# The last 48 units of a gated feed-forward layer in three PSUM banks instead of four, with TensorE adding up the four quarters of the hidden units

## The chip, the core and the metric

The kernel runs on one core of a Trainium2 chip. The metric is the device time of one execution, in microseconds (us). The kernel before takes 1150.86 us, the median of three runs from 1150.69 to 1151.08.

A core has TensorE (PE in the profile: matrix products, whose results go to PSUM, eight banks of 512 f32 columns by 128 partitions), VectorE (DVE), ScalarE (ACT), GpSimd (POOL) and DMA queues, which SyncE (SP) and GpSimd feed here. Each engine works through its own list of instructions in the order written and waits for the others by semaphores.

## What is computed

The input x has 4096 rows (2 x 2048) of 1024 f32 values. Cut to what matters:

```python
xn = layernorm(x)
# attention part: autocorrelation of each row, its 6 largest lags, softmax,
# weighted sum of the row rolled by these lags
f = rfft(xn); corr = irfft(f * conj(f)); w, delay = top_k(corr, 6)
s = sum_k softmax(w)_k * roll(xn, -delay_k)
# feed-forward part; each weight matrix is a quarter, repeated four times
lin(x, wq, A, B) = x @ tile(wq, (1, 4)).T + 0.5 * (x @ A.T) @ B.T     # LoRA of rank 2
h = silu(lin(xn, w1q, a1, b1)) * lin(xn, w3q, a3, b3)                 # 2752 units
g = silu(lin(h, w2q, a2, b2))
out = x + s * g
```

The hidden layer has 2752 units, four quarters of 688. Because w2 repeats its quarter four times, the second layer needs only the sum of the four quarters of h (688 values), and beside it the two LoRA values h @ a2.T, which need every quarter by itself.

## The kernel before

The rows are worked through in eight macros of 512 rows. Inside a macro the rows are the columns of all matrix products (512 wide), and the units are the rows. A quarter's 688 units are five chunks of 128 and a rest of 48; the chunk number c is 0 to 4, and FULL = 5 names the rest. An f32 product counts as two passes on TensorE, and the profile shows two matmuls for each.

A macro has 15 steps (STEPS). The order on every engine is written out by hand: `plan` hangs the work of the next macro's autocorrelation and of the gathers (rolled rows, fetched by GpSimd's indirect DMAs, summed by VectorE) into slots named pre, mid, half, end and between of each step, and the main loop calls them around the feed-forward code. No scheduler reorders it.

- Steps 0 to 9 (`up`): for chunk c and quarter j, a gate and an up product, each of two contraction halves (k = 0 and 1), into a bank each. A bank is seeded beforehand by ScalarE (`seed`) with the second LoRA value times its coefficient; the first LoRA value rides in the contraction itself, in row 0 of yT (gate) or yU (up), which differ in that row alone. ScalarE takes silu of the gate (L573), VectorE multiplies by the up bank (L575) into a tile z, GpSimd adds the four quarters' z into zf[c] (L578, L580).
- `a2` (L551) is LoRA's second product: for each quarter j, lhsT of 2 columns, into partitions 32j and 32j + 1 of the one bank u2. It is kept in the list `late` and issued at the next flush, one step later.
- Step 10 (`up_rest`): the rest of 48 units, below.
- Steps 11 to 14 (`down_head`, `down_tail`, twice): the output products from zf[0] to zf[4], arranged as sums and differences of blocks (`mix`, `forms`), and at the end of each half `rest` (L662): two 64-row products that add zf[5], which holds the rest's sum and the LoRA values, once in partitions 0 to 63 and again in 64 to 127. `out` follows: silu, product with s, addition of x, output DMA.

The rest before: each quarter j has its own bank of 128 rows. Rows 0 to 63 belong to the gate and 64 to 127 to the up product; of each 64, two are empty at the top, 48 are units and the others are zero. The contraction half k = 1 is the same input for both, so one 128-column product (L597) does it. Half k = 0 takes yT for the gate and yU for the up product, so it is two 64-column products into the two halves of the bank (L604). Quarters 0 and 1 come first, then the flush (a2 of chunk 4) and the slots mid and half (the next macro's last spectrum products), then quarters 2 and 3, and then four silus (L614) and four products on 64 partitions (L615). GpSimd adds three quarters (L619, L620). `a2` of the rest (64 rows, 2 columns, four quarters) is flushed in `down_head`.

`lora_mid`, at the end of step 11, finishes zf[5]: VectorE adds the fourth quarter (L625), then four times half a row pair of u2 into rows 0 and 1 (L627), and ScalarE copies the 64 rows into the upper partitions (L630). In that slot it stands behind the next macro's `again` and `lora_spread`, whose ScalarE copies are L278, L264, L272 and L273, after the TensorE product L262.

Seeds of the rest: two ScalarE instructions on 64 rows for each bank (L539), eight in a macro. The banks of `full` rotate through five buffers, shared by the gate and up banks, the rest's banks and the output banks y. The lines that say how a rest bank is seeded and used:

```python
            if c == FULL:
                acc = full(f"gu_{self.m}_{c}_{j}")
                for wi in range(2):
                    at = slice(64 * wi, 64 * wi + 64)
                    nc.scalar.activation(acc[at, :], self.st.second[at, wi, :], AF.Copy, scale=b5_sb[at, j : j + 1])
```

Of the kernel before, what the change touches and what calls it, by code (L numbers as in the profile page):

```python
# [35 lines left out]
F32 = mybir.dt.float32  # L36
U32 = mybir.dt.uint32
I32 = mybir.dt.int32
AF = mybir.ActivationFunctionType
ALU = mybir.AluOpType  # L40
# [4 lines left out]
Q2 = H // 4  # L45
TOP = 6
EPS = 1e-5
P = 128
RT = 4
NR = RT * P  # L50
NC = 6
# [4 lines left out]

FULL = 5
REST = Q2 - FULL * P
QF = FULL * P

MID = 2 * FULL
# [7 lines left out]
def block_kernel(ctx: ExitStack, tc: tile.TileContext, x, w13t, w0t, w5t, w2t, a13, b13, b5, a2t, tf, ti, pick, out):  # L69
    nc = tc.nc  # L70
    rows = x.shape[0]
# [6 lines left out]
    const = pool("const", 1)  # L78
# [3 lines left out]
    p5 = pool("p5", ROLLS)  # L82
# [21 lines left out]
    tf_sb = const.tile([P, 8, P], F32)  # L104
    ti_sb = const.tile([P, 4, NL], F32)
    w13_sb = const.tile([P, FULL, 8, 2, P], F32)
    w5_sb = const.tile([P, 2, 4, P], F32)
    w2_sb = const.tile([P, NC, L], F32)
    t_sb = const.tile([P, 3, 2, 512], F32)
    b5_sb = const.tile([P, 4], F32)  # L110
    b13_sb = const.tile([P, FULL, 8], F32)
    a2_sb = const.tile([P, 4 * NC, 2], F32)
    a13_sb = const.tile([P, 8, 32], F32)
    pick_sb = const.tile([P, P], F32)

# [24 lines left out]
    def lessen(w, w0):  # L140

        nc.vector.scalar_tensor_tensor(w(0), w0, minus, w(0), ALU.mult, ALU.add)
        nc.gpsimd.tensor_tensor(w(1), w(1), w0, ALU.subtract)
# [338 lines left out]
    class Gathers:  # L482
# [3 lines left out]
        def add(self, st, r):  # L486
            self.ready += [(st, r, k) for k in range(TOP)]
# [30 lines left out]
    class Ffn:  # L518
# [13 lines left out]
        def seed(self, i, which=(0, 1)):  # L532

            c, j = divmod(i, 4)
            if c == FULL:
                acc = full(f"gu_{self.m}_{c}_{j}")
                for wi in range(2):
                    at = slice(64 * wi, 64 * wi + 64)
                    nc.scalar.activation(acc[at, :], self.st.second[at, wi, :], AF.Copy, scale=b5_sb[at, j : j + 1])  # L539
                self.accs[i] = acc  # L540
            if c >= FULL:
                return
            for wi in which:
                acc = full(f"gu_{self.m}_{c}_{j}_{wi}")
                q = 2 * j + wi
                nc.scalar.activation(acc, self.st.second[:, wi, :], AF.Copy, scale=b13_sb[:, c, q : q + 1])  # L546
                self.accs.setdefault(i, []).append(acc)

        def a2(self, c, zs, rows):
            for j, z in enumerate(zs):  # L550
                nc.tensor.matmul(  # L551
                    self.u2[32 * j : 32 * j + 2, :], lhsT=a2_sb[:rows, 4 * c + j, :], rhs=z[:rows, :],
                    start=(c == 0), stop=(c == FULL),
                )

        def flush(self):
# [3 lines left out]
        def up(self, c, pair, mid, half):  # L560
            zs, st = self.zs.setdefault(c, []), self.st
            for jj in range(2):
                j = 2 * pair + jj
                accs = self.accs.pop(4 * c + j)
                for wi, acc in enumerate(accs):
                    for k in range(2):
                        y = (st.yT[:, 0, :], st.yU)[wi] if k == 0 else st.yT[:, 1, :]
                        nc.tensor.matmul(  # L568
                            acc, lhsT=w13_sb[:, c, 2 * j + wi, k, :], rhs=y, start=False, stop=(k == 1),
                            skip_group_check=True,  # L570
                        )
                z = p5.tile([P, NR], F32, tag="z", name=f"z_{self.m}_{c}_{j}")
                nc.scalar.activation(z, accs[0], AF.Silu)  # L573
                self.seed(4 * c + j + 2)
                nc.vector.tensor_tensor(z, z, accs[1], ALU.mult)  # L575
                zs.append(z)
                if j == 1:
                    nc.gpsimd.tensor_tensor(self.sum_of(c), zs[0], zs[1], ALU.add)  # L578
                elif j > 1:
                    nc.gpsimd.tensor_tensor(self.zf[c], self.zf[c], z, ALU.add)  # L580
                if jj == 0:
                    self.flush()
                    mid()
                    half()
            if pair == 1:
                self.late.append(lambda: self.a2(c, zs, P))

        def up_rest(self, mid, half):

            st = self.st  # L590
            self.seed(4 * FULL + 2)
            self.seed(4 * FULL + 3)
            accs = [self.accs.pop(4 * FULL + j) for j in range(4)]
            for pair in range(2):
                js = (2 * pair, 2 * pair + 1)
                for j in js:
                    nc.tensor.matmul(  # L597
                        accs[j], lhsT=w5_sb[:, 1, j, :], rhs=st.yT[:, 1, :], start=False, stop=False, skip_group_check=True
                    )

                for j in js:
                    for wi, y in enumerate((st.yT[:, 0, :], st.yU)):
                        at = slice(64 * wi, 64 * wi + 64)
                        nc.tensor.matmul(  # L604
                            accs[j][at, :], lhsT=w5_sb[:, 0, j, at], rhs=y, start=False, stop=True, skip_group_check=True
                        )
                if pair == 0:
                    self.flush()
                    mid()
                    half()  # L610
            zs = self.zs[FULL] = []
            for j, acc in enumerate(accs):
                z = p5.tile([P, NR], F32, tag="z", name=f"z_{self.m}_{FULL}_{j}")
                nc.scalar.activation(z[:64, :], acc[:64, :], AF.Silu)  # L614
                nc.vector.tensor_tensor(z[:64, :], z[:64, :], acc[64:, :], ALU.mult)  # L615
                zs.append(z)
            self.late.append(lambda: self.a2(FULL, zs, 64))
            last = self.sum_of(FULL)
            nc.gpsimd.tensor_tensor(last[:64, :], zs[0][:64, :], zs[1][:64, :], ALU.add)  # L619
            nc.gpsimd.tensor_tensor(last[:64, :], last[:64, :], zs[2][:64, :], ALU.add)  # L620

        def lora_mid(self):

            last, z = self.zf[FULL], self.zs[FULL][3]
            nc.vector.tensor_tensor(last[:64, :], last[:64, :], z[:64, :], ALU.add)  # L625
            for j in range(4):
                nc.vector.scalar_tensor_tensor(  # L627
                    last[0:2, :], self.u2[32 * j : 32 * j + 2, :], 0.5, last[0:2, :], ALU.mult, ALU.add
                )
            nc.scalar.copy(last[64:, :], last[:64, :])  # L630

        def mix(self, a):
# [174 lines left out]
    def load_first(c):  # L807
        w0 = first_times[c] = p3.tile([P, 8, P], F32, tag="s", name=f"w0_{c}")
        if c < FULL:
            nc.sync.dma_start(w0, bass.AP(w0t.tensor, w0t.offset + c * 8 * P, [[0, P], [P, 8], [1, P]]))  # L810
        else:
            nc.sync.dma_start(w0[:, :4, :], bass.AP(w0t.tensor, w0t.offset + c * 8 * P, [[0, P], [P, 4], [1, P]]))

    def lessen_part(c):
        w0 = first_times.pop(c)
        if c < FULL:
            lessen(lambda k: w13_sb[:, c, :, k, :], w0)
        else:
            lessen(lambda k: w5_sb[:, k, :, :], w0[:, :4, :])


    with tc.manual_schedule():
# [70 lines left out]


        st.lora_first(ffns[0])
        for m in range(macros):
            ffn = ffns[m]
            ffn.start()
            pre, mid, half, end, sums, between = plan(m, corrs[m], corrs[m + 1], corrs[m + 2], gathers, ffns[m + 1])
            for p in range(STEPS):  # L900
                for f in pre[p]:
                    f()
                gathers.begin()
                middle = lambda p=p: [f() for f in mid[p]]

                def others(p=p):
                    gathers.sum(sums[p][0])
                    if sums[p][0]:
                        gathers.begin()
                    for f in half[p]:  # L910
                        f()

                if p < MID:
                    ffn.up(p // 2, p % 2, middle, others)
                elif p == MID:
                    ffn.up_rest(middle, others)
                else:
                    q, part = divmod(p - MID - 1, 2)
                    if part == 0:
                        ffn.down_head(q, middle, others)  # L920
                    else:
                        s = lambda i, q=q: gathers.whole(m, 2 * q + i)
                        ffn.down_tail(middle, others, s, lambda p=p: [f() for f in between[p]])
                gathers.sum(sums[p][1])
                for f in end[p]:
                    f()
# [111 lines left out]
```

## Time and profile before

| | us |
|---|---|
| median of three runs | 1150.86 |
| profiled execution | 1149.63 |
| its span (first to last instruction) | 1147.6 |
| mean granted TensorE clock | 0.993 of full speed |
| TensorE busy | 1110.5 |
| VectorE busy | 832.1 |
| GpSimd busy | 718.7 |
| ScalarE busy | 617.4 |

The two passes of an f32 product appear as two matmuls. In the profile's timeline each line gives the start, the length, the engine, the line of the kernel, the operation, the tile written and the tiles read, the shape of the weights (rows*columns) and the count of instructions merged. The profile draws a matmul from its start until its last result is written, so that neighbours overlap: how fast TensorE goes is read from the distance of starts.

The costliest lines on TensorE are L568 (the chunks' gate and up products) and L652 (the output products). The lines of the rest are small: L597 x64 (30.2 us), L604 x128 (30.9 us in shared passes), and L551 on the rest x64 (8.3 us).

### The profile page before, as it was taken

How to read it: one execution, taken by the hardware profiler on the slowest of the kernel's cores; microseconds unless marked ns; L12 is line 12 of the kernel's file. 1: busy time of each engine (PE TensorE's matmuls, PEld its weight loads, DVE VectorE, ACT ScalarE, POOL GpSimd, SP SyncE). 2: the span in 40 equal slices, each digit the busy share in tenths (PEclk: the TensorE clock that was granted, in tenths of full speed). 3: DMA queues.
4: the chain of work that ended last, by engine and by line, in shares of the span. 5: the costliest groups of instructions: out<-in, count | busy, mean ns of one | idle time of the engine just before them, and what ended most of it. 6: DMA issues, size and time to landing. Idle time of an engine off the chain costs nothing.

```text
span 1147.6 us, 11271 instructions
## 1 busy us (share of the span) xinstructions
PE 1110.5 (97%) x3476; PEld 472.8 (41%) x3476; DVE 832.1 (73%) x1213; ACT 617.4 (54%) x1077; POOL 718.7 (63%) x607
## 2 busy tenths in 40 slices
PE   5988799999999999999999999999999999999997
PEld 4433234443444434444344443444344443444432
DVE  5689788777777777778767777777777777763563
ACT  4736453666437663476635665366643766345541
POOL 4577774778366773578635784567836677356832
PEclk9998999999999999999999999999999999999999
DMA  9942555565355652556435663555635565154533
GB/s 363 417 142 74 165 174 172 186 212 200 109 176 204 214 183 67 194 207 214 157 101 204 218 201 101 167 179 207 199 110 176 202 218 180 52 182 131 160 95 119
DMA packets 64915, 201.77 MB, mean 176 GB/s; under 512 B 7612, under 2 KB 7868, under 8 KB 64088
## 3 DMA queue, kind: packets, MB, share of 16 engines
q0 software_dynamic: 27648, 100.68, 28.1%
q1 hardware_dynamic: 37208, 100.39, 24.0%
q8 instruction: 27, 0.44, 0.1%
q14 instruction: 32, 0.26, 0.1%
HBM read 150.65 MB, written 50.39 MB: 175 GB/s over the span
## 4 chain that ended last, share of the span: by engine, by line
PE 86%; DVE 4%; POOL 4%; issue 3%; DMA 1%; ACT 1%; SPq 0%; DVEq 0%; POOLq 0%; ACTq 0%
PE gu L568 44%; PE y L652 19%; PE u L551 4%; PE y L662 3%; PE gu L604 2%; PE gu L597 2%; PE t L234 2%; PE fe L385 1%; PE fo L385 1%; PE o L432 1%; PE fe L388 1%; PE e L432 1%; PE fo L388 1%; PE ua L250 1%; DMA x<-in_x 1%
## 5 line engine op out<-in xcount | busy, mean ns | idle before, releaser
L568 PE MATMUL gu<-yT,w_sb 128*128 128x512 f32 x960 | 461.4, 602 | 1.4 <-ACT gu L546 1.4
L568 PEld LDWEIGHTS gu<-yT,w_sb 128*128 128x128 f32 x960 | 177.0, 191 | 236.2 <-issue 211.7
L493 POOL DMA_INDIRECT roll<-scr,lag x192 | 233.4, 1216 | 42.8 <-issue 30.3
L515 DVE SCALAR_TENSOR_TENSOR s<-roll,w,s 128x1024 f32<-128x1024 f32 x160 | 229.1, 1432 | 5.0 <-DMA roll<-scr,lag 4.1
L546 ACT ACTIVATE gu<-second,b_sb 128x512 f32<-128x512 f32 x320 | 208.4, 685 | 9.6 <-DVE z L575 8.0
L575 DVE TENSOR_TENSOR z<-z,gu 128x512 f32<-128x512 f32 x160 | 108.9, 683 | 116.9 <-PE gu L568 80.4
L580 POOL TENSOR_TENSOR zf<-zf,z 128x512 f32<-128x512 f32 x80 | 129.5, 1619 | 67.1 <-DVE z L575 66.1
L573 ACT ACTIVATE z<-gu 128x512 f32<-128x512 f32 x160 | 95.1, 594 | 141.6 <-PE gu L568 138.8
L568 PE MATMUL gu<-yU,w_sb 128*128 128x512 f32 x320 | 163.4, 592 | 0.0
L468 POOL TENSOR_TENSOR e<-euler,e 128x6 f32<-128x6 f32 x32 | 49.6, 1549 | 150.2 <-DVE e L467 135.4
L652 PE MATMUL y<-w_sb,zf 128*128 128x512 f32 x256 | 122.1, 599 | 0.0
L734 POOL TENSOR_TENSOR x<-g,x 128x512 f32<-128x512 f32 x62 | 81.4, 1322 | 61.6 <-DVE g L733 37.5
L568 PEld LDWEIGHTS gu<-yU,w_sb 128*128 128x128 f32 x320 | 61.1, 191 | 77.4 <-issue 69.9
L578 POOL TENSOR_TENSOR zf<-z,z 128x512 f32<-128x512 f32 x40 | 64.8, 1621 | 29.9 <-DVE z L575 29.6
L733 DVE TENSOR_TENSOR g<-s,g 128x512 f32<-128x512 f32 x64 | 52.7, 853 | 39.5 <-ACT g L732 38.7
L732 ACT ACTIVATE g<-y 128x512 f32<-128x512 f32 x64 | 35.4, 593 | 73.5 <-PE y L662 40.8
L652 PEld LDWEIGHTS y<-w_sb,zf 128*128 128x128 f32 x256 | 46.2, 190 | 59.8 <-issue 59.0
L450 ACT COPY corr<-corr 128x511 f32<-128x511 f32 x32 | 19.8, 617 | 85.2 <-DVE corr L449 85.2
L652 PE MATMUL y<-w_sb,S 128*128 128x512 f32 x128 | 61.8, 605 | 0.0
L652 PE MATMUL y<-t_sb,zf 128*128 128x512 f32 x128 | 60.2, 592 | 0.0
L210 DVE TENSOR_TENSOR a<-x 128x512 f32<-128x512 f32 x28 | 34.9, 1246 | 26.2 <-ACT x L203 26.2
L551 PE MATMUL u<-z,a_sb 128*2 128x512 f32 (+1 forms) x384 | 50.9, 591 | 0.5 <-DVE z L575 0.5
(181 smaller groups left out, 1534.1 us busy)
## 6 DMA issues: line engine op xcount, KB each, us to landing
scr<-x SPq DMA_DIRECT2D x64, 512.0 KB
x<-in_x SPq DMA_DIRECT2D x32, 512.0 KB
x<-in_x SPq DMA_DIRECT2D x64, 256.0 KB
out<-x SPq DMA_DIRECT2D x64, 256.0 KB
w_sb<-in_w13t SPq DMA_DIRECT2D x5, 1024.0 KB
second<-rows SPq DMA_DIRECT2D x14, 256.0 KB
w_sb<-in_w2t SPq DMA_DIRECT2D x1, 3072.0 KB
roll<-scr,lag POOLq DMA_INDIRECT x192, 5.2
```

Source lines behind the costliest of these rows:

```text
L493: nc.gpsimd.indirect_dma_start(out=g, out_offset=None, in_=st.scratch[r].rearrange("p (n o) -> (p n) o", o=1), in_offset=bass.IndirectOffs ...
L515: nc.vector.scalar_tensor_tensor(s, g, w, s, ALU.mult, ALU.add)
L546: nc.scalar.activation(acc, self.st.second[:, wi, :], AF.Copy, scale=b13_sb[:, c, q : q + 1])
L551: nc.tensor.matmul(self.u2[32 * j : 32 * j + 2, :], lhsT=a2_sb[:rows, 4 * c + j, :], rhs=z[:rows, :], start=(c == 0), stop=(c == FULL),)
L568: nc.tensor.matmul(acc, lhsT=w13_sb[:, c, 2 * j + wi, k, :], rhs=y, start=False, stop=(k == 1), skip_group_check=True,)
L573: nc.scalar.activation(z, accs[0], AF.Silu)
L575: nc.vector.tensor_tensor(z, z, accs[1], ALU.mult)
L578: nc.gpsimd.tensor_tensor(self.sum_of(c), zs[0], zs[1], ALU.add)
L580: nc.gpsimd.tensor_tensor(self.zf[c], self.zf[c], z, ALU.add)
L652: nc.tensor.matmul(acc, lhsT=lhs, rhs=rhs, start=(first and a == 0), stop=True, skip_group_check=True)
L733: nc.vector.tensor_tensor(g, s(i)[:, cols], g, ALU.mult)
L734: (nc.vector if last else nc.gpsimd).tensor_tensor(xt, g, xt, ALU.add)
```

## The change

The 48 units of all four quarters are dealt out anew. The first 32 of each quarter (HEAD) make 4 x 32 = 128 rows: one full bank for the gate and one for the up product. The last 16 of each quarter (TAIL) make 64 rows: the gate's in partitions 0 to 63 and the up product's in 64 to 127 of a third bank. So there are three banks, `gate`, `up` and `last`.

`up_rest` does gate and up with four full products, then silu on 128 rows and one VectorE product into the tile `head`; then the flush and the slots as before; then `last` with one full product and two 64-column ones, silu and product on 64 rows into `tail`.

The quarters are no longer added by GpSimd. LoRA's second product for the rest (`a2_rest`) is two products of 64 columns: head (128 rows) into partitions 0 to 63 of u2, tail (64 rows) into 64 to 127. Besides the two LoRA columns, their weights hold a 2.0 for each unit in the column of its sum; all of a2_sb is scaled by 0.5 once, at setup, by ScalarE. To have all of u2's 128 rows written, `a2` on chunk 0 has 32 columns for each quarter instead of 2, with zeros in the others. Tile shapes on TensorE, as the program has them: 128 rows by 64 columns for head, 64 by 64 for tail, 64 by 32 for each of the four products before.

`lora_mid` becomes: ScalarE copies the upper half of u2 into zf[5], VectorE adds the lower half of u2 to it, ScalarE copies the result into the upper partitions. Rows 32 and 33 of each 64 now carry the LoRA values of other quarters, so w2's rows for the rest hold b2 twice.

Seeds: one ScalarE instruction each for gate and up, two for `last`. Loads: a2 grows from 24 to 144 KB, w5 shrinks from 512 to 384 KB, its correction w0 from 256 to 192 KB.

```diff
+HEAD = 32
+TAIL = REST - HEAD
...
-    w5_sb = const.tile([P, 2, 4, P], F32)
+    w5_sb = const.tile([P, 2, 3, P], F32)
...
-    a2_sb = const.tile([P, 4 * NC, 2], F32)
+    a2_sb = const.tile([P, 288], F32)
...
-            if c == FULL:
+            if c == FULL and j < 3:
                 acc = full(f"gu_{self.m}_{c}_{j}")
-                for wi in range(2):
-                    at = slice(64 * wi, 64 * wi + 64)
+                for wi, at in ((0, slice(0, 64)), (1, slice(64, P))) if j == 2 else ((j, slice(0, P)),):
                     nc.scalar.activation(acc[at, :], self.st.second[at, wi, :], AF.Copy, scale=b5_sb[at, j : j + 1])
...
-        def a2(self, c, zs, rows):
+        def a2(self, c, zs):
             for j, z in enumerate(zs):
+                n, at = (32, 32 * j) if c == 0 else (2, 4 * 32 + 8 * (c - 1) + 2 * j)
                 nc.tensor.matmul(
-                    self.u2[32 * j : 32 * j + 2, :], lhsT=a2_sb[:rows, 4 * c + j, :], rhs=z[:rows, :],
-                    start=(c == 0), stop=(c == FULL),
+                    self.u2[32 * j : 32 * j + n, :], lhsT=a2_sb[:, at : at + n], rhs=z,
+                    start=(c == 0), stop=True, skip_group_check=True,
+                )
+
+        def a2_rest(self, zs):
+
+            for z, rows, at in zip(zs, (P, 64), (0, 64)):
+                nc.tensor.matmul(
+                    self.u2[at : at + 64, :], lhsT=a2_sb[:rows, 160 + at : 224 + at], rhs=z[:rows, :],
+                    start=False, stop=True, skip_group_check=True,
                 )
...
-            st = self.st
+            st, c = self.st, FULL
             self.seed(4 * FULL + 2)
-            self.seed(4 * FULL + 3)
-            accs = [self.accs.pop(4 * FULL + j) for j in range(4)]
...
+            gate, up, last = [self.accs.pop(4 * FULL + j) for j in range(3)]
+            times = (st.yT[:, 0, :], st.yU)
...
+            for wi, acc in enumerate((gate, up)):
+                add(acc, w5_sb[:, 1, wi, :], st.yT[:, 1, :])
+                add(acc, w5_sb[:, 0, wi, :], times[wi])
+            nc.scalar.activation(head, gate, AF.Silu)
+            nc.vector.tensor_tensor(head, head, up, ALU.mult)
+            self.flush()
+            mid()
+            half()
+            add(last, w5_sb[:, 1, 2, :], st.yT[:, 1, :])
+
+            for wi in range(2):
+                at = slice(64 * wi, 64 * wi + 64)
+                add(last[at, :], w5_sb[:, 0, 2, at], times[wi])
+            nc.scalar.activation(tail[:64, :], last[:64, :], AF.Silu)
+            nc.vector.tensor_tensor(tail[:64, :], tail[:64, :], last[64:, :], ALU.mult)
+            self.late.append(lambda: self.a2_rest((head, tail)))
...
-            last, z = self.zf[FULL], self.zs[FULL][3]
-            nc.vector.tensor_tensor(last[:64, :], last[:64, :], z[:64, :], ALU.add)
-            for j in range(4):
-                nc.vector.scalar_tensor_tensor(
-                    last[0:2, :], self.u2[32 * j : 32 * j + 2, :], 0.5, last[0:2, :], ALU.mult, ALU.add
-                )
+            nc.scalar.copy(last[64:, :], self.u2[64:, :])
+            nc.vector.tensor_tensor(last[:64, :], self.u2[:64, :], last[64:, :], ALU.add)
             nc.scalar.copy(last[64:, :], last[:64, :])
...
         st.lora_first(ffns[0])
+
+        nc.scalar.activation(a2_sb, a2_sb, AF.Copy, scale=0.5)
```

More of the change, by code (lines that the diff above doesn't have):

```diff
@@ L106, in block_kernel @@
     w13_sb = const.tile([P, FULL, 8, 2, P], F32)
-    w5_sb = const.tile([P, 2, 4, P], F32)
+    w5_sb = const.tile([P, 2, 3, P], F32)
     w2_sb = const.tile([P, NC, L], F32)
     t_sb = const.tile([P, 3, 2, 512], F32)
-    b5_sb = const.tile([P, 4], F32)
+    b5_sb = const.tile([P, 3], F32)
     b13_sb = const.tile([P, FULL, 8], F32)
-    a2_sb = const.tile([P, 4 * NC, 2], F32)
+    a2_sb = const.tile([P, 288], F32)
     a13_sb = const.tile([P, 8, 32], F32)
@@ L585, in up @@
             if pair == 1:
-                self.late.append(lambda: self.a2(c, zs, P))
+                self.late.append(lambda: self.a2(c, zs))
         def up_rest(self, mid, half):
-            st = self.st
+            st, c = self.st, FULL
             self.seed(4 * FULL + 2)
-            self.seed(4 * FULL + 3)
-            accs = [self.accs.pop(4 * FULL + j) for j in range(4)]
[L594 to L598, printed above, removed]
-                    )
[L601 to L617, printed above, removed]
-            last = self.sum_of(FULL)
-            nc.gpsimd.tensor_tensor(last[:64, :], zs[0][:64, :], zs[1][:64, :], ALU.add)
@@ L620, in up_rest @@
-            nc.gpsimd.tensor_tensor(last[:64, :], last[:64, :], zs[2][:64, :], ALU.add)
-        def lora_mid(self):
-            last, z = self.zf[FULL], self.zs[FULL][3]
-            nc.vector.tensor_tensor(last[:64, :], last[:64, :], z[:64, :], ALU.add)
-            for j in range(4):
-                nc.vector.scalar_tensor_tensor(
-                    last[0:2, :], self.u2[32 * j : 32 * j + 2, :], 0.5, last[0:2, :], ALU.mult, ALU.add
-                )
+            gate, up, last = [self.accs.pop(4 * FULL + j) for j in range(3)]
@@ new lines, in up_rest @@
+            times = (st.yT[:, 0, :], st.yU)
+            add = lambda acc, lhs, y: nc.tensor.matmul(
+                acc, lhsT=lhs, rhs=y, start=False, stop=True, skip_group_check=True
+            )
+            head, tail = [p5.tile([P, NR], F32, tag="z", name=f"z_{self.m}_{c}_{j}") for j in range(2)]
+            for wi, acc in enumerate((gate, up)):
+                add(acc, w5_sb[:, 1, wi, :], st.yT[:, 1, :])
+                add(acc, w5_sb[:, 0, wi, :], times[wi])
+            nc.scalar.activation(head, gate, AF.Silu)
@@ L630, in lora_mid @@
+        def lora_mid(self):
+            last = self.sum_of(FULL)
+            nc.scalar.copy(last[64:, :], self.u2[64:, :])
+            nc.vector.tensor_tensor(last[:64, :], self.u2[:64, :], last[64:, :], ALU.add)
             nc.scalar.copy(last[64:, :], last[:64, :])
@@ L811, in load_first @@
         else:
-            nc.sync.dma_start(w0[:, :4, :], bass.AP(w0t.tensor, w0t.offset + c * 8 * P, [[0, P], [P, 4], [1, P]]))
+            nc.sync.dma_start(w0[:, :3, :], bass.AP(w0t.tensor, w0t.offset + c * 8 * P, [[0, P], [P, 3], [1, P]]))
     def lessen_part(c):
@@ L818, in lessen_part @@
         else:
-            lessen(lambda k: w5_sb[:, k, :, :], w0[:, :4, :])
+            lessen(lambda k: w5_sb[:, k, :, :], w0[:, :3, :])
     with tc.manual_schedule():
@@ L978 @@
     b13 = np.ascontiguousarray(b[1].transpose(2, 0, 1))
-    w5 = np.zeros((P, 2, 4, P), f32)
-    for name, to in (("w1q", 2), ("w3q", 66)):
-        w5[..., to : to + REST] = v[name].reshape(4, Q2, P, 2)[:, QF:].transpose(2, 3, 0, 1)
-    w0[FULL, :4] = w5[0, 0]
-    w5[0, 0] = 0
+    w5 = np.zeros((P, 2, 3, P), f32)
+    b5 = np.zeros((2, 3, P), f32)
+    for wi, (wn, bn) in enumerate((("w1q", "b1"), ("w3q", "b3"))):
+        w = v[wn].reshape(4, Q2, P, 2)[:, QF:].transpose(2, 3, 0, 1)
+        b = v[bn].reshape(4, Q2, 2)[:, QF:].transpose(2, 0, 1)
+        w5[:, :, wi] = w[..., :HEAD].reshape(P, 2, P)
+        w5[:, :, 2, 64 * wi : 64 * wi + 64] = w[..., HEAD:].reshape(P, 2, 64)
+        b5[:, wi] = b[..., :HEAD].reshape(2, P)
+        b5[:, 2, 64 * wi : 64 * wi + 64] = b[..., HEAD:].reshape(2, 64)
+    w0[FULL, :3] = w5[0, 0]
+    w5[0, 0] = b5[0]
+    b5 = np.ascontiguousarray(b5[1].T)
     w2t = np.zeros((P, NC, L), f32)
@@ L988 @@
     for to in (0, 64):
-        w2t[to : to + 2, FULL] = v["b2"].T
-        w2t[to + 2 : to + 2 + REST, FULL] = v["w2q"].T[QF:]
+        for at in (0, 32):
+            w2t[to + at : to + at + 2, FULL] = v["b2"].T
+        w2t[to + 2 : to + 32, FULL] = v["w2q"].T[QF : QF + 30]
+        w2t[to + 34 : to + 52, FULL] = v["w2q"].T[QF + 30 :]
     a13 = np.zeros((P, 4, 8, 4), f32)
@@ L1009 @@
     pick = np.zeros((P, P), f32)
-    b5 = np.zeros((P, 4), f32)
-    a2t = np.zeros((P, 4 * NC, 2), f32)
-    b1, b3 = (v[k].T.reshape(2, 4, Q2) for k in ("b1", "b3"))
+    a2t = np.zeros((P, 288), f32)
     for i in range(4):
@@ L1017 @@
             pick[32 * g + np.arange(4), at + (np.arange(4) ^ own)] = 1.0
-        for b, to in ((b1, 2), (b3, 66)):
-            w5[0, 0, i, to : to + REST], b5[to : to + REST, i] = b[:, i, QF:]
     a2 = v["a2"].T.reshape(4, Q2, 2)
     for j in range(4):
-        for c in range(FULL):
-            a2t[:, 4 * c + j] = a2[j, c * P : (c + 1) * P]
-        a2t[2 : 2 + REST, 4 * FULL + j] = a2[j, QF:]
+        a2t[:, 32 * j : 32 * j + 2] = a2[j, :P]
+        for c in range(1, FULL):
+            at = 4 * 32 + 8 * (c - 1) + 2 * j
+            a2t[:, at : at + 2] = a2[j, c * P : (c + 1) * P]
+        for i in range(REST):
+            first = i < HEAD
+            row = HEAD * j + i if first else TAIL * j + i - HEAD
+            at = 160 if first else 224
+            a2t[row, at : at + 2] = a2[j, QF + i]
+            a2t[row, at + (2 + i if i < 30 else 4 + i)] = 2.0
     tf, ti = _tables()
```

## The prediction

> **What bounds the kernel now.** I read the page's busy table first, then the chain that ended last, then TensorE's own timeline in a middle macro (the fourth of eight), and last ScalarE's, VectorE's and TensorE's where the changed sums are used.
>
> ```profile
> PE 1110.5 (97%) x3476; PEld 472.8 (41%) x3476; DVE 832.1 (73%) x1213; ACT 617.4 (54%) x1077; POOL 718.7 (63%) x607
> ...
> PE 86%; DVE 4%; POOL 4%; issue 3%; DMA 1%; ACT 1%; SPq 0%; DVEq 0%; POOLq 0%; ACTq 0%
> ```
>
> The first line is busy time by engine, the second the chain's shares. Both name TensorE. Busy matmuls can still hide gaps, because each is drawn 0.59 us long while a new one starts every 0.43 us, so the starts decide. TensorE's timeline of that macro, from the last units to LoRA's second product (start, length, line, count; each f32 matmul is two passes):
>
> ```profile
> 560.29 1.88 PE L597 MATMUL gu<-yT,w_sb 128*128 128x512 f32 x4
> 562.10 0.64 PE L604 MATMUL gu<-yT,w_sb 128*64 128x512 f32 x1
> ...
> 563.97 1.04 PE L551 MATMUL u<-z,a_sb 128*2 128x512 f32 x8
> ...
> 566.76 1.88 PE L597 MATMUL gu<-yT,w_sb 128*128 128x512 f32 x4
> 568.57 0.64 PE L604 MATMUL gu<-yT,w_sb 128*64 128x512 f32 x1
> 568.58 0.64 PE L604 MATMUL gu<-yU,w_sb 128*64 128x512 f32 x1
> 569.05 0.59 PE L604 MATMUL gu<-yT,w_sb 128*64 128x512 f32 x1
> 569.06 0.59 PE L604 MATMUL gu<-yU,w_sb 128*64 128x512 f32 x1
> 569.48 0.59 PE L604 MATMUL gu<-yT,w_sb 128*64 128x512 f32 x1
> ...
> 569.91 0.59 PE L604 MATMUL gu<-yT,w_sb 128*64 128x512 f32 x1
> ...
> 570.44 1.99 PE L652 MATMUL y<-w_sb,zf 128*128 128x512 f32 x4
> 572.26 1.88 PE L652 MATMUL y<-t_sb,zf 128*128 128x512 f32 x4
> 573.98 1.88 PE L652 MATMUL y<-t_sb,S 128*128 128x512 f32 x4
> 575.78 1.04 PE L551 MATMUL u<-z,a_sb 64*2 64x512 f32 x8
> 576.75 0.49 PE L432 MATMUL o<-ti_sb,bT 128*128 128x129 f32 x2
> ```
>
> Three things are to be seen. Nothing waits: 572.26 to 573.98 is four passes at 0.43 us, and the macro period (first L597 to first L597) is 136.2 us from the second macro on. Two 64-column matmuls share a pass: starts 568.57 and 568.58. And each change of tile shape costs: the last 128x128 pass before a 64-column one takes 0.52 us (560.29 to 562.10 is 3 x 0.43 + 0.52), the first 64-column pass 0.48 (568.57 to 569.05), the last one 0.53 (569.91 to 570.44). So a pass taken from TensorE is worth its 0.43 us until something else comes late.
>
> **The last units (up_rest), per macro.** Before, each of its two halves is two full products (4 passes) and two pairs of 64-column products (4 shared passes): 560.29 to 563.97 and 566.76 to 570.44, 3.68 us each. After, the first half is four full products: 7 x 0.43 + 0.52 into L551's shape = 3.53 us, 0.15 less. The second half is one full product and one pair: 0.43 + 0.52 + 0.48 + 0.53 = 1.96 us, 1.72 less. Together 1.87 us, by eight macros 15.0. In the first macro TensorE afterwards stands 1.6 us for VectorE (L398 frees the odd bank at 156.7), and that wait eats the 0.15: 14.8 in all.
>
> **LoRA's second product on the last units, per macro.** Before, four 2-column products of one shape (64 rows) share each pass: 575.78 to 576.75, 0.97 us. After there are two: head has 128 rows and 64 columns, tail 64 rows and 64 columns. Their columns do not meet, but their shapes differ, and no row of this trace has two shapes in one pass. Lower bound: they share, like the pair above, 0.48 + 0.53 = 1.01, so +0.04. Upper bound: every pass alone, 0.59 us long with its 64-column weights in front (0.14 us by the L604 load's group): 4 x 0.73 = 2.92, so +1.95. Between: head and tail one after the other at the pace and the shape changes above: 0.48 + 0.52 + 0.48 + 0.53 = 2.01, so +1.04. I take +1.04, because at every shape change in this trace the new shape starts only after the old one's pass is through, and every shared pass is of one shape; by eight 8.3 us, bounds +0.3 and +15.6.
>
> The Trainium skill, page "TensorEngine Tiling (Array Packing)", section Key Properties, says that a change of tiling mode, not merely of tile, drains TensorE. The trace agrees as far as it goes: the 0.09 us extra at each change is its row. By that rule the two products do not overlap; by the pair's row alone they do, and the time would be 8.0 us lower.
>
> **LoRA's second product on the first units** writes 32 columns instead of 2. The L250 products have 32 columns, and they too go four to a pass; their weights load in 110 ns against 81, under the pass before. Nothing.
>
> **What leaves the other engines, per macro.** ScalarE: four of eight seeds (0.69 each) and two of four silus (0.59), plus one copy (0.6): 3.3 us less. VectorE: four products, an add and four LoRA adds (L615, L625, L627, 0.67 to 0.69 each) become two products and one add: 4.1 less. GpSimd: L619 and L620, 2.7 less. I count none of it as gain, since TensorE's starts show no wait for them here. SP's and GpSimd's queues keep their order and issues.
>
> **The new chain (lora_mid).** It was five VectorE steps and a ScalarE copy; it is a ScalarE copy, a VectorE add and the old copy. ScalarE does its first one behind the copies of the next macro's LoRA:
>
> ```profile
> 582.45 0.58 ACT L273 COPY yU<-u 1x512 f32<-1x512 f32 x1
> 583.53 0.62 ACT L630 COPY zf<-zf 64x512 f32<-64x512 f32 x1 [0.51 <-DVE zf L627]
> ```
> ```profile
> 586.46 1.13 PE L662 MATMUL y<-w_sb,zf 64*128 64x512 f32 x4
> 587.52 0.70 PE L652 MATMUL y<-w_sb,S 128*128 128x512 f32 x1
> ```
>
> From L273's end at 583.03: 0.62 + 0.68 + 0.62 and some hand-over is 585.0, against 584.15 now; L662 reads it at 586.46. All of these hang on TensorE's L262 a little earlier and move with it, so 1.4 us of slack is left and the cost is nothing; each 0.1 us beyond that slack costs 0.8 us in all. Behind the waiting add on VectorE stands L708, which then ends near 585.1; its reader on TensorE is at 587.52. A bound from below is nothing, as the sums are not wanted sooner.
>
> **The banks.** up_rest takes three of five banks instead of four, and head is read before the second half; the first output product then finds its bank free earlier than now. It does not wait now either, so nothing.
>
> **Setup.** One ScalarE scaling of 128x288, 0.4 us by L436 (128x258, 0.37), ahead of the first silu (35.90). ScalarE sits idle 1.1 us before the next silu at 39.30, so it is absorbed: between 0 and 0.4, I take 0. It waits for the a2 load, 144 KB instead of 24, issued at 9.55; at the page's 363 GB/s the extra is 0.3 us, and 26 us lie between. The w5 load shrinks by 128 KB and w0's last part by 64, in a stretch where DMA is not what I can show to be waited for; its correction shrinks by a quarter of 0.75 us on VectorE and of 1.29 on GpSimd, once. Bounds -0.5 and +0.4, taken as nothing.
>
> **The sum.** -14.8 + 8.3 = -6.5 us. Profiled execution: 1149.63 - 6.5 = 1143.1 (span 1147.6, 2.0 around it). It lies 1.2 below the median of the runs; against the median I predict 1150.86 - 6.5 = 1144.4.
>
> **Rivals.**
> *Head and tail share passes.* For it: disjoint columns, and the pair's two starts 0.01 us apart. Against: one shape in each shared pass seen. 1150.86 - 14.8 + 0.3 = 1136.4.
> *Every pass alone.* For it: two shapes in turn may leave nothing to overlap. Against: within a shape the passes now follow at 0.43 to 0.48. 1150.86 - 14.8 + 15.6 = 1151.7, no change.
> *Slower: the new chain comes late.* TensorE would stand at L662 in each macro. Against it: VectorE waited only 4.1 us in the whole run for gathers ahead of L515, the kind of step that stands before the add. For it: three hand-overs between two engines, behind L273. It decides at 1.4 + 0.8 = 2.2 us late, that is if the three steps take 4.1 us instead of 1.9. If they took 5.8, the wait would be 2.5 us in seven macros (the last has no L273 in front): 1144.4 + 17.5 = 1161.9.
>
> **How the numbers follow.** Serial products 0.68, shared 0.20, every pass alone 0.06, late chain 0.06. The likeliest gives 1144.4, its own range is 1142.5 to 1146.5 (alternating instead of consecutive passes adds 0.7, setup up to 0.4, the clock after the first macro's stalls some 0.5, by the passes there that take 0.85 us). The range goes down to the shared case and leaves the last two out: 1135.5 to 1147.0. About 0.2%, 2.3 us, is what a measurement of this kernel can tell from no change. Serial and shared are faster: 0.88; each pass alone is the same: 0.06; the late chain is slower: 0.06.
>
> **What would show it.** In the profile after: macro period 135.4 us (134.3 if shared); from the first full product of the second half to the first output product 1.96 us; the two products on u taking 2.0 us with tail's start some 1.0 after head's (both within 0.02 if shared); no wait of TensorE at the rest's products (L662 now). Wrong would make it: a wait there, a new wait of the next macro's seeds, or passes on u longer than 0.53.

## The result, and the profile after

The kernel after takes 1143.74 us (median of 4 runs, 1142.89 to 1145.79); the kernel before, measured beside it, takes 1150.97 us (4 runs, 1150.69 to 1151.35). The ratio is 0.9946, with a 95% interval from 0.9934 to 0.9959: 4.7 to 7.6 us faster. The forecast was 1144.4 us, by two products on u that run one after the other.

The profiled execution takes 1143.51 us against 1149.63, so 6.1 us less, where the sum said 6.5. Busy time by engine and the shares of the chain that ended last, from the page of after:

```profile
PE 1104.8 (97%) x3364; PEld 472.1 (41%) x3364; DVE 797.5 (70%) x1165; ACT 591.2 (52%) x1038; POOL 696.5 (61%) x591
...
PE 80%; POOL 5%; DVE 5%; issue 4%; DMA 3%; ACT 2%; SPq 0%; POOLq 0%; DVEq 0%; ACTq 0%
```

TensorE lost 5.7 us of busy time, which is about what the run got shorter. VectorE lost 34.6, ScalarE 26.2 and GpSimd 22.2; whether that adds to the gain is asked in e2. The chain's share of TensorE falls to 80% while TensorE stays 97% busy. I read this as a chain that passes through other engines where several end nearly together, which I did not follow up; the argument rests on TensorE's starts.

TensorE's timeline of after in the same macro as in the prediction (start, length, line, tile, shape of the weights, count). The line numbers have moved: L606 is now all products of the rest, L555 is a2, L563 a2_rest, L654 the output products and L664 the rest's products.

```profile
557.82 2.74 PE L606 MATMUL gu<-yT,w_sb 128*128 128x512 f32 x6
560.39 1.02 PE L606 MATMUL gu<-yU,w_sb 128*128 128x512 f32 x2
561.34 1.04 PE L555 MATMUL u<-z,a_sb 128*2 128x512 f32 x8
562.32 1.13 PE L392 MATMUL fe<-bT,tf_sb 128*128 128x512 f32 x2
563.28 1.02 PE L392 MATMUL fo<-bT,tf_sb 128*128 128x512 f32 x2
564.14 1.59 PE L606 MATMUL gu<-yT,w_sb 128*128 128x512 f32 x3
565.09 0.64 PE L606 MATMUL gu<-yU,w_sb 128*64 128x512 f32 x1
565.57 0.59 PE L606 MATMUL gu<-yT,w_sb 128*64 128x512 f32 x1
565.57 0.59 PE L606 MATMUL gu<-yU,w_sb 128*64 128x512 f32 x1
566.10 1.98 PE L654 MATMUL y<-w_sb,zf 128*128 128x512 f32 x4
567.92 1.88 PE L654 MATMUL y<-t_sb,zf 128*128 128x512 f32 x4
569.63 1.88 PE L654 MATMUL y<-t_sb,S 128*128 128x512 f32 x4
571.44 2.07 PE L563 MATMUL u<-z,a_sb 128*64 128x512 f32 x4
573.45 0.71 PE L436 MATMUL o<-ti_sb,bT 128*128 128x129 f32 x4
```

The first half takes 561.34 - 557.82 = 3.52 us (before 3.68), the second 566.10 - 564.14 = 1.96 (before 3.68), and the two products on u 573.45 - 571.44 = 2.01 (before 0.97). The line L563 merges both products; by shapes, and in two windows, the groups of after come apart (busy us, mean ns of one, idle before). From 571.5 to 572.4 us:

```profile
L563 PE MATMUL u<-z,a_sb 128*64 128x512 f32 x2 | 1.1, 618 | 0.0
```

and from 572.6 to 573.4 us:

```profile
L563 PE MATMUL u<-z,a_sb 64*64 64x512 f32 x2 | 1.1, 614 | 0.0
```

Head's two passes come first, tail's two behind them: tail's first starts at 572.45, 1.01 us after head's, and no pass is shared.

The macro period, from one first product of the rest to the next, is 135.37 us in most macros against 136.18, so 0.81 less. The pieces give just that: 0.16 in the first half of the rest and 1.72 in the second, less 1.04 for the two products on u and 0.03 for the 32 columns on chunk 0 (the lines of chunk 0 stand below, in the comparison with the prediction). Of the eight stretches (seven periods and the one from the last rest to TensorE's end), five gained 0.75 to 0.84, the third 1.19, the fifth 0.36 and the first 0.47.

ScalarE's timeline of after around the new chain, in the next macro's LoRA copies and lora_mid:

```profile
579.14 0.58 ACT L277 COPY yU<-u 1x512 f32<-1x512 f32 x1
579.74 0.58 ACT L630 COPY zf<-u 64x512 f32<-64x512 f32 x1
581.07 0.62 ACT L632 COPY zf<-zf 64x512 f32<-64x512 f32 x1 [0.75 <-DVE zf L631]
581.71 0.38 ACT L440 COPY oc<-o 128x258 f32<-128x258 f32 x1
```

TensorE's timeline at the reader of that chain:

```profile
583.15 1.13 PE L664 MATMUL y<-w_sb,zf 64*128 64x512 f32 x4
584.21 1.98 PE L654 MATMUL y<-w_sb,S 128*128 128x512 f32 x4
```

From L277's end (579.72) to the last copy's end (581.69) are 1.97 us, and L664 starts 1.46 us later, without a wait. In the last macro 5.0 us are left.

### The profile page after: what moved, and what is told of

It is laid out like the page before. It is cut to its first block, busy times and chain, and to the rows that moved or that the text cites. A ratio compares the mean times of both kernels' runs of the same rounds, so it can differ in the third digit from the quotient of the medians.

```text
span 1141.7 us, 10938 instructions
## 1 busy us (share of the span) xinstructions
PE 1104.8 (97%) x3364; PEld 472.1 (41%) x3364; DVE 797.5 (70%) x1165; ACT 591.2 (52%) x1038; POOL 696.5 (61%) x591
## 4 chain that ended last, share of the span: by engine, by line
PE 80%; POOL 5%; DVE 5%; issue 4%; DMA 3%; ACT 2%; SPq 0%; POOLq 0%; DVEq 0%; ACTq 0%
PE gu L580 44%; PE y L654 17%; PE gu L606 3%; PE u L555 3%; PE y L664 2%; PE t L238 2%; POOL roll L497 2%; DMA x<-in_x 2%; PE fo L389 1%; PE u L563 1%; PE fe L389 1%; DVE s L519 1%; PE fe L392 1%; PE fo L392 1%; PE o L436 1%
## 5 line engine op out<-in xcount | busy, mean ns | idle before, releaser
L654 PE MATMUL y<-w_sb,zf 128*128 128x512 f32 x256 | 122.1, 599 | 0.0
L654 PEld LDWEIGHTS y<-w_sb,zf 128*128 128x128 f32 x256 | 46.2, 190 | 59.8 <-issue 58.3
L654 PE MATMUL y<-w_sb,S 128*128 128x512 f32 x128 | 61.8, 605 | 0.1
L654 PE MATMUL y<-t_sb,zf 128*128 128x512 f32 x128 | 60.2, 592 | 0.0
L192 DVE BATCH_NORM_STATS2 stats<-x 128x6 f32<-128x512 f32 x64 | 40.8, 677 | 4.2 <-DMA x<-in_x 4.2
```

Source lines behind the costliest of these rows:

```text
L654: nc.tensor.matmul(acc, lhsT=lhs, rhs=rhs, start=(first and a == 0), stop=True, skip_group_check=True)
```

## Experiments

Four kernels (e1, e2, e4, e5) were measured beside 15 runs of the kernel before with median 1149.72 us, two (e3, e6) beside 9 with 1150.21. Since these medians differ from 1150.97 by about 1 us, ratios are compared below, and periods of the profiles where the difference is small. My theory: TensorE's passes and shape changes set the gain, and head and tail stand one behind the other because their shapes differ. The rivals: 64-column products are slow whatever their shape, the relief of the other engines plays a part, or the new chain is nearer to the path than the slack says.

**e1: head and tail in one shape.** The tail's product also takes 128 rows; the added rows of its weights are zeros, and its silu fills all 128 partitions of the operand.

```diff
-            for z, rows, at in zip(zs, (P, 64), (0, 64)):
+            for z, rows, at in zip(zs, (P, P), (0, 64)):
...
-            nc.scalar.activation(tail[:64, :], last[:64, :], AF.Silu)
+            nc.scalar.activation(tail, last, AF.Silu)
```

> The changed kernel with one difference: tail's product in LoRA's second step also has 128 rows (its silu fills all 128 partitions; the weights of the upper 64 rows are zero), so that head and tail have the same tile shape of 128 rows by 64 columns. Theory (shape is what keeps them apart): the two share passes, 1.01 us instead of 2.01 in each macro, 8.0 us less than the changed kernel's 1143.7: 1135.7, ratio to the kernel before 0.987; the macro period falls from 135.4 to 134.4. Rival (they are apart for another reason, such as both writing the one bank u2): nothing moves, 1143.7, ratio 0.994.

Measured: 1135.05 us (1134.47 to 1137.09), ratio 0.9876, interval 0.9861 to 0.9891, where after has 0.9946. TensorE's timeline of e1:

```profile
566.65 1.88 PE L654 MATMUL y<-t_sb,S 128*128 128x512 f32 x4
568.46 1.08 PE L563 MATMUL u<-z,a_sb 128*64 128x512 f32 x4
569.47 0.71 PE L436 MATMUL o<-ti_sb,bT 128*128 128x129 f32 x4
```

The same four passes now take 569.47 - 568.46 = 1.01 us instead of 2.01, and the period is 134.38 instead of 135.37. The longer contraction costs nothing: two shared passes and their shape changes took 0.48 + 0.53 = 1.01 us in the kernel before too. In both kernels the products write the same halves of u2 from the same number of columns; only the rows differ. So it is the unequal number of rows that keeps the two products apart, and 64 columns are not slow in themselves.

**e5: unequal shapes at another place.** The two 64-column products of the rest's last bank share their passes. Here one of them gets 64 rows instead of 128, which leaves out half of a contraction half of the up product for the last 16 units.

```diff
-                add(last[at, :], w5_sb[:, 0, 2, at], times[wi])
+                rows = slice(0, (P, 64)[wi])
+                add(last[at, :], w5_sb[rows, 0, 2, at], times[wi][rows, :])
```

> The changed kernel, but in up_rest the up product of the pair of 64-column products on the third bank takes 64 rows of its contraction instead of 128 (the other 64 rows of that half are left out of the sum for the last 16 units). Less arithmetic, same number of instructions, but two shapes in the pair. Theory (a change of shape keeps products apart): the pair takes 2.0 us instead of 1.0 in each macro, 8 us more: 1151.7, ratio to before 1.001. Rival (what keeps head and tail apart is something of u2 and not the shape): 1143.7, ratio 0.994.

Measured: 1151.63 us (1150.01 to 1152.68), ratio 1.0015, interval 1.0006 to 1.0025. TensorE's timeline of e5, in the second half of the rest:

```profile
567.33 2.02 PE L606 MATMUL gu<-yT,w_sb 128*128 128x512 f32 x4
569.28 1.07 PE L606 MATMUL gu<-yU,w_sb 64*64 64x512 f32 x2
570.28 1.98 PE L655 MATMUL y<-w_sb,zf 128*128 128x512 f32 x4
```

The first line merges the full product's two passes with the two of the 64-column product that keeps its 128 rows; the second is the other one. 570.28 - 567.33 = 2.95 us instead of 1.96, though less is computed. The period is 136.36, 0.99 more. In another bank than u2 and with other operands, unequal rows cost the same 1.0 us that e1 gained, and they take away the whole gain of the change.

**e2: the removed work of the other engines put back.** Per macro four seeds, two silus, two products, two GpSimd additions and the four two-row LoRA additions, all written into the tile zf[5] before `lora_mid` fills it, so that TensorE's work stays as in after. The work is the old one in kind and amount, not in its operands: apart from the LoRA additions it reads and writes no PSUM bank.

```diff
+            spare = self.sum_of(FULL)
+            for _ in range(4):
+                nc.scalar.activation(spare[:64, :], st.second[:64, 0, :], AF.Copy, scale=0.5)
...
+            for _ in range(2):
+                nc.scalar.activation(spare[64:, :], st.second[64:, 1, :], AF.Silu)
+            for _ in range(2):
+                nc.vector.tensor_tensor(spare[:64, :], tail[:64, :], head[:64, :], ALU.mult)
+            for _ in range(2):
+                nc.gpsimd.tensor_tensor(spare[:64, :], tail[:64, :], head[:64, :], ALU.add)
...
-            last = self.sum_of(FULL)
+            last = self.zf[FULL]
+            for j in range(4):
+                nc.vector.scalar_tensor_tensor(
+                    last[0:2, :], self.u2[32 * j : 32 * j + 2, :], 0.5, last[0:2, :], ALU.mult, ALU.add
+                )
```

> The changed kernel with the work that left the other engines put back as idle work into zf[5] before it is written: per macro four ScalarE seeds and two silus on 64 rows, two VectorE products on 64 rows and four two-row LoRA adds, two GpSimd adds. TensorE is untouched. Theory (only TensorE's passes count): as the changed kernel, 1143.7, ratio to before 0.994, at most 0.5 us more. Rival (part of the gain is relief of VectorE, 4.1 us per macro): a part of 7 us comes back, 1146 or more, and TensorE shows waits at the output products' second column half.

Measured: 1143.71 us (1142.89 to 1144.28), ratio 0.9949, interval 0.9935 to 0.9962. Busy time on the page of e2:

```profile
PE 1103.7 (97%) x3364; PEld 472.2 (41%) x3364; DVE 826.9 (72%) x1213; ACT 620.7 (54%) x1086; POOL 722.7 (63%) x607
```

VectorE, ScalarE and GpSimd are back near their times of before, the period is 135.37 as in after, and the slack in front of the rest's products still 1.47 us in seven macros. So the gain of the change is TensorE's, and taking 83 us off the other three engines bought nothing that the interval can tell.

**e3 and e4: the chain made longer.** The last copy of lora_mid is repeated, three times in all (e3) or six times (e4). A copy behind a copy stands 0.65 us later, so the chain ends 1.3 or 3.25 us later, on either side of the 1.46 us of slack. Lines behind the edit move by one: the last copy is L633, the rest's products are L665.

```diff
-            nc.scalar.copy(last[64:, :], last[:64, :])
+            for _ in range(3):
+                nc.scalar.copy(last[64:, :], last[:64, :])
```

> The changed kernel with the last ScalarE copy of lora_mid done three times instead of once: 2 x 0.65 = 1.30 us more in the chain, less than the 1.47 us of slack. Theory (the slack is what hides the chain): 0.17 us of slack are left and the time is the changed kernel's, 1143.7 beside a kernel before of 1151.0, ratio 0.994; the macro period stays at 135.4. Rival (the five further copies cost time by keeping ScalarE from other work, not through the slack): two fifths of the 13.7 us that those cost come back here too, 1149, ratio 0.999.

Measured: 1143.70 us (1142.10 to 1144.02), ratio 0.9939, interval 0.9924 to 0.9954: no different from after. ScalarE's timeline of e3, and then TensorE's:

```profile
582.07 1.91 ACT L633 COPY zf<-zf 64x512 f32<-64x512 f32 x3 [0.75 <-DVE zf L631]
584.01 0.37 ACT L440 COPY oc<-o 128x258 f32<-128x258 f32 x1
```
```profile
583.21 1.02 PE L655 MATMUL y<-w_sb,zf 128*128 128x512 f32 x2
584.16 1.13 PE L665 MATMUL y<-w_sb,zf 64*128 64x512 f32 x4
585.22 1.98 PE L655 MATMUL y<-w_sb,S 128*128 128x512 f32 x4
```

The copies end at 583.98, the products start at 584.16: 0.18 us are left, and nothing is lost (period 135.37). This execution reached the second macro's rest 1.0 us later than after did, but not by the chain, which has 0.17 us left there: the granted clock was 0.55 of full speed from 157.0 to 160.6 us, where after has 1.00, and the first lengthened chain runs later, from 175.65.

> The changed kernel with the last ScalarE copy of lora_mid done six times instead of once, 5 x 0.62 = 3.1 us more between the VectorE add and the rest's products that read it. Theory (1.47 us of slack, measured between that copy's end and L664 in seven macros, 5.0 in the last): TensorE waits 3.1 - 1.47 = 1.6 us in seven macros, 11.4 us in all: 1155, ratio to before 1.004. Rival (the chain is hidden much deeper, since TensorE could be held by something else there): 1143.7, ratio 0.994.

Measured with six copies: 1157.37 us (1156.57 to 1158.79), ratio 1.0066, interval 1.0050 to 1.0081; I expected 1155. ScalarE's timeline of e4, and then TensorE's:

```profile
587.36 3.86 ACT L633 COPY zf<-zf 64x512 f32<-64x512 f32 x6 [0.75 <-DVE zf L631]
591.25 0.38 ACT L440 COPY oc<-o 128x258 f32<-128x258 f32 x1
```
```profile
589.45 1.12 PE L665 MATMUL y<-w_sb,zf 64*128 64x512 f32 x2
591.27 1.12 PE L665 MATMUL y<-w_sb,zf 64*128 64x512 f32 x2 [0.71 <-ACT zf L633]
```

The chain now ends 3.25 - 1.46 = 1.79 us after the moment at which the products would start, and the period grows by 1.82 us, to 137.19. Seven such macros make 12.7 us. The first macro lost 0.84 us more and the fifth 1.25. The chain is no later there; the granted clock was 0.58 from 157.0 to 160.6 us in the first and from 729.5 to 733.0 in the fifth, where after has 1.00 in both stretches. Why the clock fell just there stays open. The forecast of 1155 had these two stretches at nothing, and a further copy at 0.62 us instead of 0.65. The timeline also shows how the wait works: the product of the lower 64 rows, whose operand is there, goes alone at 589.45; that of the upper rows comes 1.82 us later. The pair that shares its passes when both operands are ready no longer does, so the early half saves nothing.

**e6: the pair of 64 columns next to the products of 2 columns.** e1, and besides the last bank's products of the rest moved ahead of the flush, so that TensorE goes from 128 columns to 64, to 2 and back to 128, three shape changes instead of four.

```diff
-            self.flush()
-            mid()
-            half()
             add(last, w5_sb[:, 1, 2, :], st.yT[:, 1, :])
...
+            self.flush()
             nc.scalar.activation(tail, last, AF.Silu)
             nc.vector.tensor_tensor(tail[:64, :], tail[:64, :], last[64:, :], ALU.mult)
+            mid()
+            half()
```

> The changed kernel with tail's product on 128 rows and, in up_rest, the third bank's products moved ahead of the flush (LoRA's second product of chunk 4) and of the next macro's last spectrum products, so that the 64-column pair and the 32-column products follow each other with one change of shape less. Theory (each change of shape costs its own 0.1 to 0.15 us): the macro period falls from 134.4 to 134.2 or 134.3, some 1.1 us in all; and in the first macro the wait of 1.7 us for VectorE before the second spectrum product shrinks, because 1.9 us of TensorE's work now stand before it: together some 2.8 us less than with the tail's shape alone, 1132.3, ratio to before 0.985. Rival (VectorE's spectrum sums now come later, and the lag products behind the output products wait for them): the period grows above 134.4 and TensorE shows a wait at the lag products.

Measured: 1131.37 us (1130.98 to 1133.05), ratio 0.9840, interval 0.9827 to 0.9854. It is the fastest of all, 1.6% below the kernel before. TensorE's timeline of e6:

```profile
556.47 0.64 PE L606 MATMUL gu<-yU,w_sb 128*64 128x512 f32 x1
556.94 0.59 PE L606 MATMUL gu<-yT,w_sb 128*64 128x512 f32 x1
556.95 0.59 PE L606 MATMUL gu<-yU,w_sb 128*64 128x512 f32 x1
557.47 1.04 PE L555 MATMUL u<-z,a_sb 128*2 128x512 f32 x8
558.44 1.12 PE L392 MATMUL fe<-bT,tf_sb 128*128 128x512 f32 x2
559.40 1.02 PE L392 MATMUL fo<-bT,tf_sb 128*128 128x512 f32 x2
560.26 1.88 PE L654 MATMUL y<-w_sb,zf 128*128 128x512 f32 x4
561.98 1.88 PE L654 MATMUL y<-t_sb,zf 128*128 128x512 f32 x4
```

The period is 134.18 us against 134.38 in e1, so the change of shape that was saved was worth 0.20. Half of it lies behind the change: the first four output products' passes take 561.98 - 560.26 = 1.72 us here, where they follow 128 columns, and 1.82 in after (566.10 to 567.92), where they follow 64. The rest of e6's gain comes from the first macro, where after and e1 wait for VectorE. TensorE's timeline there, first after, then e6:

```profile
153.80 1.12 PE L392 MATMUL fe<-bT,tf_sb 128*128 128x512 f32 x2
156.49 1.12 PE L392 MATMUL fo<-bT,tf_sb 128*128 128x512 f32 x2 [1.56 <-DVE bT L402]
157.45 1.59 PE L606 MATMUL gu<-yT,w_sb 128*128 128x512 f32 x3
```
```profile
155.66 1.12 PE L392 MATMUL fe<-bT,tf_sb 128*128 128x512 f32 x2
156.62 1.02 PE L392 MATMUL fo<-bT,tf_sb 128*128 128x512 f32 x2
157.48 1.88 PE L654 MATMUL y<-w_sb,zf 128*128 128x512 f32 x4
```

fo starts at nearly the same time in both, but in e6 the rest's 1.9 us of products have been done by then: they stand in what was the wait. The first period falls from 136.61 us in e1 to 134.42. With about 0.20 in nearly all the others that is the 3.6 us by which the span is shorter (1129.6 against 1133.2); I had expected 2.8.

## Why the prediction was right, point by point

- **TensorE's passes set the time.** Right: e2 shows that the relief of the other engines is worth nothing that can be measured, and e1 and e5 that 1.0 us of TensorE per macro is worth 1.0 us of period.
- **The last units, 3.53 and 1.96 us.** Measured 3.52 and 1.96. Passes at 0.43 us and the shape changes of before (0.52, 0.48, 0.53) hold in an order that the trace of before did not have. They are not the whole price of a change of shape: e6 shows 0.10 us more in the passes that follow it. The kernels before and after both pay that in front of the same products (1.82 us for the first four output passes in both), so the sum did not miss it.
- **LoRA's second product, +1.04.** Measured 2.01 - 0.97 = 1.04. Here the choice between serial and shared decided 8 us. The stated range took in both, so that the time lies in it says little of the mechanism; tail's start 1.01 us after head's does. What it rested on, that every shared pass in the trace was of one shape, was borne out by taking the difference of shapes away (e1) and by making one elsewhere (e5). The other reason, that a new shape starts only after the old one's pass is through, was read too strictly: by the drawn lengths the 64-column pass at 562.10 starts 0.07 us before the end of the pass in front (560.29 + 1.88). What the trace shows is a start 0.52 us behind the last one, not beside it. The Trainium skill's rule, page "TensorEngine Tiling (Array Packing)", section Key Properties, that a change of tiling mode drains TensorE, agrees: 2.01 us with two shapes, 1.01 with one. The rival with shared passes gave 1136.4 us, 0.9874 of the kernel before; e1, which makes them share, measured 0.9876.
- **The new chain, 1.4 us of slack.** Measured 1.46 to 1.47 us, and e3 and e4 show from both sides that it is real. The rival that ends slower would have needed the three steps to take 4.1 us; they took 1.97.
- **LoRA on chunk 0 with 32 columns, nothing.** Slightly wrong. TensorE's timeline of before, and then of after:

```profile
221.23 1.04 PE L551 MATMUL u<-z,a_sb 128*2 128x512 f32 x8
222.20 1.99 PE L568 MATMUL gu<-yT,w_sb 128*128 128x512 f32 x4
```
```profile
220.72 1.06 PE L555 MATMUL u<-z,a_sb 128*32 128x512 f32 x8
221.72 1.98 PE L580 MATMUL gu<-yT,w_sb 128*128 128x512 f32 x4
```

  It takes 1.00 us instead of 0.97, 0.2 us in eight macros. That the longer weight load is behind it was not tried.
- **The first macro's wait eats 0.15.** Only in part: VectorE released the odd bank 0.24 us earlier than before, which the sum had at nothing. The macro still gained 0.47 where the sum has 1.72 - 1.04 = 0.68, because small waits of 0.1 to 0.2 us, 0.42 together, turned up near 207 and 216 us that before does not have.
- **The sum.** The eight stretches add up to 6.0 us: 0.2 of the missing 0.5 is the 32 columns, 0.2 the first macro. The two macros with 1.19 and 0.36 nearly cancel (before lost some 0.4 in the third, after in the fifth). What remains is under 0.1 us, which I leave open. The profiled execution is 6.1 us shorter, and the measured interval of 4.7 to 7.6 takes in both 6.1 and 6.5.

## What to carry to other kernels

Where TensorE's starts follow without gaps, count its passes by the distance of starts and price an edit by passes and shape changes alone; work taken off other engines was worth nothing here, where no wait showed it. Small products that are meant to run side by side should have the same number of rows: in both places tried here, 128 beside 64 rows did not share a pass, and in e1 padding one with zero rows cost nothing and gave 1.0 us per pair. Unequal numbers of columns were not tried. How much slack a chain has is best learnt by making it longer in two steps, one to each side of what the trace says.

## What the runs showed that I had not expected

- More was to be had from the same idea than the change took: padding tail's product (e1) gave about 8 us more by the ratios (8.5 by the spans), and one change of order (e6) 3.6 us more by the spans.
- A pair that shares passes has no use of its early half when the other's operand is late (e4): the wait is lost whole, 1.82 us for a chain 1.79 late.
- Moving 1.9 us of TensorE's work in front of a product that waited 1.6 us for VectorE (e6) removed that wait, which the prediction had taken as given.
